# Maxima turned in one piece, phases summed with heads on partitions, the shared expert beside the logits, and another order table, in a two-layer block on one core

## Chip, core and metric

The kernel runs on one core of a Trainium2 chip. The metric is device time in microseconds (us); a median of runs is compared. Everything below in us is from the profiled execution unless it is said to be of the runs.

## What is computed

Sixteen sequences of 512 tokens with 128 features go through two layers, each an attention-like part and a mixture of experts, with a layer norm after each part. The reference, cut to what matters here:

```python
# layer 0, first part, for each of 16 heads
p1 = sum(sin(a1 * n + b1) * c, axis=-2)          # phases: 64 sines per head, 512 positions
p2 = sum(sin(a2 * n + b2) * c, axis=-2)
cross, diag, extra = exp(clip(x@k1 + p1)), exp(clip(x@k2)), exp(clip(x@k3))
num = cumsum(cross * values) * exp(p2) * extra + values * diag
den = cumsum(cross) * exp(p2) * extra + diag
x = layernorm(x + einsum(num / den, output_weight))
# layer 0, second part: the best of 8 experts per token, relu; layernorm
# layer 1, first part: 16 heads of 8 features
logits = q @ k.T * scale + pos_bias               # softmax, values, output; layernorm
# layer 1, second part
shared_out = swiglu(x, shared_gate, shared_up, shared_down)
top_id, score = argmax(x @ gate_w.T), sigmoid(max(x @ gate_w.T))
routed_out = swiglu of expert top_id on x * score
x = layernorm(x + shared_out + routed_out)
```

## The kernel before

**A list of operations and an order table.** The kernel first lists some 6,200 operations (`op(engine, cost, emit, reads, writes, delay)`), each for one engine, with the buffers that it reads and writes. `Plan.order` (L243) then runs them on a clock of its own: each engine starts the ready operation with the smallest key whose buffers are free. The key is read from `ORDER`, a string with two characters for each operation; `cost` and `delay` say how long an operation holds its engine and how long its readers wait after it. The result is the order in which instructions are emitted, engine by engine, and every engine's queue keeps that order. The costs have no other effect on the chip.

**Buffers.** Each kind of buffer has a fixed count (L331 to L365): three "pair" buffers of two PSUM banks, two "one" buffers of one bank, and in SBUF six "w2", five "p", three "mid" and eight "x", among others.

**Stages.** Sequences are taken in chunks of 2, 3, 4, 4, 2 and 1 (`CHUNKS`). For a chunk, layer 0 runs per sequence (`attention0`, with one `tile0` for each 128 tokens), then `mixture0` (logits, `route` on VectorE, a scatter of tokens into a list in DRAM, slots of 128 tokens with the weights of their expert fetched by GpSimd, a gather). Layer 1 of a chunk (`attention1`, `mixture1`) runs while layer 0 of the next chunk fills the gaps.

**Phases** (`phases`, L471). For p1 and for p2, 1024 angles (8 times 128, on partitions) times 512 positions are made in four quarters. For a quarter, ScalarE and VectorE make the angle (L484, L478), ScalarE rounds the number of turns (L491, L494), VectorE takes the turns off and clips (L499, L502), ScalarE takes the sine (L511). After all four quarters, TensorE sums: 4 blocks of positions times 8 angle blocks, with the sines as the weights and 16 columns of coefficients moving (L520), so that positions end up on partitions.

**Bias** (`slide`, L568). From a distance table a line of 1024 biases per head is made (L582 to L610), written to DRAM, and read back with every partition shifted by one (the "slid" rows, L627, 448 KB for each of 16 heads); a product turns each around (L636).

**Attention of layer 1** (`attention1`). A sequence has four groups of four heads. `spread` (L1265) sends queries and keys of a group into padded tiles: four transfers of bf16 rows and four of f32 rows. `maxima` makes rounded scores (L1286 adds the bias, L1293 the products) and takes their row maxima (ScalarE copies at L1308, VectorE halves and reduces at L1316 and L1317) into `tops[g % 2]`, of 128 queries times 4 blocks times 4 heads. `shifted` sends the negated maxima into one row of the padded queries, so that the exact scores come out shifted. `weighted` makes the exact scores (L1359), adds the bias (VectorE, L1374), takes the exponential (ScalarE, L1380), and multiplies with the values (L1389). `shifted` reads:

```python
def turn():
    for it in range(NT):
        nc.tensor.transpose(pm()[:NG, col(it)], tops[g % 2][:, it, :], ident)
# PE turn; ACT copies pm[:4, :512] to mx; then one transfer on SP:
nc.sync.dma_start(qk_pad[g % 2][D1 :: 32, 0, :], mx()[:NG])
```

**Second mixture** (`mixture1`, L1483). After `route`, GpSimd scales the tokens and scatters them; then, for each sequence of the chunk, the tokens are turned again (`transposed`, L687 and L690), go through the shared expert (L1519, `swiglu` at L1466 to L1478, L1528), are added to x (L1536) and are stored to the output (L1543). The routed experts follow in `slots` (L1554, L962, L1566), and the gathered result is added to what is read back from the output (L1578, L1583).

**Queues.** SP issues all plain transfers in order; GpSimd issues the scatters, the gathers and the fetches of weights, in order with its own arithmetic. A transfer that waits holds up all that stands behind it on its queue.

Of the kernel before, what the change touches and what calls it, by code (L numbers as in the profile page):

```python
# [18 lines left out]
P = 128  # L19
# [33 lines left out]
    "###$#P#8#N#R#H#1#6#<#B#Q#.#0#4#>#L#?#3#A#J#W#@#/#F#U#[#_#i#O#9#T#]#a#Y#Z#^#b#c#d#e#h#q#v#g#k#o#u"  # L53
    "#|$$$*$,#)#&#*#l#~$##z#y#n#}#p#I#V#`#G#E#%#,#-#S#(#M#D#X#m#s$/$2$5#w$&$;$+$1$8$@$D$G$I$K#t$-$A$F"
    "$J$N$O$P$X$]$b$e$H$T$Y$^$f$j$k$o$v$z%3%7$_$d$g$m${$~%#%&%*%-%2%8%>%@%E%I%L%O#r#K#'$i$n$p$t$y$|$}"
    "%%%(%)%.%/%0%6%:%<%A%1%4%5%;%B%F%G%J%N%P%R%V%?%C%D%K%U%X%Y%]%`%b%h%k%Q%S%T%Z%c%f%g%j%n%t%z%|&%&)"
    "&,&-&.&0&1&2&8&=&D&U&3&6&;&a&:&l&p&t&y'#')',&b'-&|'$'@'C'F'J'L&r'M'O'T'`'f'j'n'o'''p'q'u(&(+(2(5"
    "(7(=(N(Q(Z(^(O(_(e(l(t#:#2#5#7#;#C#f#j$r%$%'$E$U$Z#{$%$.$)$:$>$B$M$R$L$[$`$a$l$s$3$=$C$S$q$w$'$6"
    "$9$($7$<#x$0$4$?$Q$V$x%H%M$u%9%=$W$c$h&$%v%y#=(a(c(m(y(f(r(u(k(p(x)#(s(w)$).({):)l)o)b)k){)])a)-"
    ")3)m)5);)9)?)I)@)C)0)7)O*)*/*1)+)6)')2)%)8)/)4*J*M*R*Q*U*Y)B)F)D)J)T*o*t*x*s*u*z)H)M)K)P)Z*y*|*~"  # L60
    "*}+$+,)W)^)Q)V)d+#+*+/+&+++2)_)g)U)Y)w)}*#*'+5+9+@)p)q)i)j+'+-+)+(*T*[*_*W*Z*h*L*P*:*A*S*f*i*l*j"
    "*q*v*8*<*4*9*C+0+3+8+6+:+D*+*0)~***6+7+B+H+;+A+L*>*D*%*-*G*`*d+4+Q+V+Z)e)c)X)[+C+>+?+<+G+N+T+S+X"
    "+b)z*&*2*5*;+Y+_+a+`+d+h)u)y)r)v*(+e+k+p+g+m+{*B*F*]*a*e+x+|,$+~,',+)x)|)n)t*,+J+M+O,/,4,7+n+r+v"
    "+q+s,@,(,,,1,0,3,J,5,:,>,F,M,`,E,L,S,R,W,c,f,{-#-7-C-I-R-U-Y-g-j-n.,.4+},%-]-d,.,<,6,;,8,V,T,=,D"
    ",A,C,Q,K,r,w,x,~-(-+-0,a,d-9,p,s,X,_,y,k,o-3-<-D-T-^-a,H,I,?,Y,[,O,N,U-l-p-t-s-w-},v,z,|-'-1-x.#"
    ".+.&.-.0,],b,g,j,m.*.1.6...2.;-$-,---5-?.7.<.C.B.F.R,i,l,n,q,u-G-N-P.W.^.b-2-/-8-;.:.@.?.=.D.H.L"
    ".K.S.c-E-J-~.%.).T.[.a.Y.].h-@-F-X-`-i._.i.m.f.j.y-V-Z-M-S-b.k.s.x.o.t/(-c-h-_-f-m.9.>.J/+/2/8-)"
    "-*-6-4.u.p.q.r.v.z.}.|/$/*-:->-B-H-L/%/)/-/,///5-=-A-Q-W-[/7/;/>/</@/D.'./-u-|.5/A/E/I/H/L/R-o-r"
    "-K-O-y.P.V.~/V/`/c/./1/6/4/9/G/J/N/Q/P/T/[/U/X/Z/Y/b/h/a/g/j/i/m/q/v/x/|00070C0T0`0f0k0v0x0~1&%+"
    "%,%W%[%^%_%a%d%e%i%l%m%q%r%s%x%~&&&+%p%u%{&(&/&4&5&9&>&A&G&L&#&'&*&7&<&?&@&C&J&N&S&W&B&F&O&R&X&["  # L70
    "&^&`&c&i&m&o&s&v'('+'.'1%o%w%}&E&H&I&K&M&Q&P&T&]&V&Y&Z&_&g&j&x&{&d&h&k&q&z&}&~'&'*'/'8'>&n&u&w'%"
    "'4':';'?'B'E'['a'0'3'6'='D'G'H'K'P'W']'b'e'h'w'z'|(#&e&f'2'5'7'9'<'A'I'N'X'U'Y'Z'_'d'i't'x'R'V'^"
    "'c'm'r's'v'y'}(-(3'g'k'l'{(*(.(/(1(6(:(;(@'~(%(((0(9(<(>(A(C(J(U(V(](d(j(o(q(z(})()1)A)L)f*$)&))"
    ")G*=)=*H*K*b*g+R+W+[*?+]+f+i+t+y,9,B,^*N,G,t,}-e-k-q-v-z+l-{.$.(.G.N.X.`.d-%.e.g.l.{/&/:/?/B/O/l"
    "/p/t/z/f0%0*010@/y090G0O0Y151<1A1O1=1@1F1[1C1q1W1_1x2)1{2'20282;2>1H1P2,2:21272@2r2w2x2*1K22252Q"
    "2]2V2Z2a3,33362&323T3V3f4%3k3n404L4P4S264Q5$5(5w695}6&6@787=7B3Y:j6b6i;#;&;';);+;/;3;5;A;`;h;i;m"
    ";s;x;S;j;w;|;~<)<,#+/~0$050=0&0-020.0/06080A030D0Q0J0:0M0V0X0^0d0o0u0w1#1(0_0h0S0Z0s0I0P0[0a0n12"
    "171:0>0U0R0N0H0?0B0K1u1w1z1y2#2%0y1'0q0z1,1}2+2.2$2(2/0c0m0l0p0{24292<2=2A2K1+111)1-1;2B2D2I2H2P"
    "2U0g0j1.191J1S1X1]2Y2c2f0t0r0}0|2F2G2E2J2O2T2^2W2[2p1G1M1D1I1U2e2j2o2i2k2y181>1N1Y1g2l2s2u2q2t3)"
    "141B1?1E1^2v2z3$3#3&311$1*1L1R1b1o1t2S35393?101/16132{2|3%2~3'3*3.3-303O1V1e1`1c1j343;3A383=3U1Q"  # L80
    "1T1l1p1|3H3K3L3R3X3d1d1h1f1k1s3Q3[3_3W3]3j1r1v1Z1a2-2?2b3+3m4#4)3a3g3i3h3p443r3w3}3|4(494/474=45"
    "484A5?5C5I5G5L5T5Y5d5i5l5o5r5y5~6%64676;6?6C3^3e3l3q3o3s3t3y3v4-4*4.3~433z3x3{4O4T4>4E4W4J4M4F4I"
    "4N4m4q4R4V4x4i4n4U4Z4s5,51534$4,4&415F5H5B5D5J5N5P5O5U5p4v4|4_4c5&5V5]5_5^5b6'4D4G4b4g4l5j5u5{5s"
    "5v60464:4<4?4C6#6*6/6.62654H4K4]4`4d595>5Q686A6D4r4p4Y4[6(6,6-6)63666<6:6>6H4}5%4o4u5/6E6I6L6K6O"
    "6Z5'5*4t4w556S6W6]6a6f6j50565-525<6g6v6{6r6x7+575:5m5q5z6U6Y6[70717>4{4z4f4h6o6k6p6m757:7A797;7F"
    "6J6N6_6c6h7<7C7J7@7D7M6|7#6q6u7-7I7K7P7O7T7W6P6T6X6`6e7U7Y7^7]7c7y7/736d6l7H7L7N7Q8#8+827e7k7r7p"
    "7w7}7s8$8*7z8&8-8'8,808.838881858>8;8@8C8G8K8N8O8W8`8h8m8r8y9+9/929F7X7[7_7f7a7l7n7j7g7m7o7~7q8%"
    "7u7x7t8R8e8A8D8i8=8J8M8T8^8V8Z8?8B8d8E8P848:8U8n8s8w7{7|8)8(8789868<9-969A91989E90938p8v9:9C9G9L"
    "9J9P9V8H8L8c8g8q9K9O9R9Q9U9_8j8z8[8a9#9S9]9d9b9f9j9&9*8l8o9.9H9I9M9p9t9v8Y8]8S8Q9Y9[9a9W9e9h9m9k"
    "9y9~8}9'9)9,9>9z9}:&:#:-:9979;999=9B:0:8:=:5:;:@9<9@9g9i9n:>:G:J:B:H:V9l9q9o9s9x9|:%:':[:`:e9594"  # L90
    "8x8u:C:F:D:A:X:_:f:Z:b:r:$:)9r9w:,:g:l:n:m:q:w:(:+:.:1:<:o:u:z:s:v;,:6:?:I:M:Q:y:|:~:};%;8:O:S:L"
    ":P:U:Y:^:a;=;L;O;2;:;?;7;<;N;>;C;E;D;H;P;F;K;R;Q;U;X;V;Z;_;];c;e;g;k;n;p;r;u;}<%<*<-</<0<1<2'S'Q"
    "($('()(,(4(8(?(B(G(H(L(M(P(R(S(W([(D(I(K(Y(b(g(h(n(v(~)N)S(T(X(`(i(|),)*)<*E*I*O*X*.*3*7*@*V*^*c"
    "*k*m+o+u+w+z,&,e,h-&-.(F(E)>)E)R)`)h)s*r*w*{+=+E+F+K+P+U,P,Z+%+.+1+I,#,*,),2.3.8.n.w+^+c+j,-.M.Z"
    ".Q.U/0/3/e/o/=/C/F/K/k/s/w0#0'0;0E0L0W0]0b0e0i1%*p*n.A.E.I.O/#/'/M/S/]/W/^/_/d/n/r/{0)0,040<0F1i"
    "1m1n232X2_2h2n/u/}0+1~2C2M2N2R373:3B3I2`2d2g2m2}3(3/3>3F3u4'4+424;4@4B4e4k0(2L3<3@3E3G3M3P3J3N3S"
    "3Z3b3`3c5)5.5A5K4X4^4a4j4y4~5#5+5;5@5[5c54585=5E5`5e5f5n5t5x5|6$5M5S5X5h6+616=6B6F6M6Q6R6V6^6n6s"
    "6t6y6z6~7'72777R7h8/7%7(7d8F7E8X8_8f8k8t8|9$8I9%8{8~9?9D9N9T9^8b9X9Z9`9u9{:*:/:29(:3:4:7:R:W:c:h"
    ":k9c;4:t:x;J;M;T;W;Y::;a;[;b;q;v;{<#<&<.<B<E<I<P<?<R<V<c<n<X<r<z=g=n='=H>(>->2<3<4<8<=<5<6<9<O<<"
    "<j<7=L<><A<C<G<H<J<N<a<k<o<K<M<Q<S<U<Z<]<i<x<~<:<;<@<L<D<F<T<Y<_<`=j=<=w=}>/>=>6>9>B>F>J>N=i>K>I"  # L100
    ">M>y?6?#?.?;?R?Y?Z>$?X?L?OB#C$B)B/C+C4C;C=>QC:CGCQC}DlD'D*DtESEYE]?SI2F.F9IJIMIOIQIRITI[I_IgJ4J;"
    "JCJKJPJTJ>NwO%O-O7OCOML&O)O?ONOQOlOp<W<[<q<w<^<g<e<b<d<l<y<f<h=0=/=2<m=B=F=8=A=K=1=7<v<}=?=-=4=$"
    "=+=9=U=X<|=&=u>'>.>1=#=*<u<s<{=%=,<t>V>[>_>^>b>e=E=I=J=O=[>`>d>g>f>j>o=G=M=6=:=R>t>z>}>w>{?-=W=_"
    "=N=T=d>~?%?+?*?/?3=]=b=@=C=k=q=x={?7?:?>=Z=Y=>==?'?&?,?)?0?5?9?8?<?A=m=p=z>#>,???B?G?E?I?N=t=y>+"
    ">0>5?H?M?T?Q?V?`>:>>=|>&>E?W?c?g?]?f?k>L>R>A>D>U>Y>]?4?n?}@(=c=a=S=Q?^?_?d?b?h?l?p?o?r?y=o=s=e=l"
    "=~?s?w?{?v?x@$>)>3>4>8><?|@%@)@#@'@->h>l=`=f>q@*@.@1@7@:@?>%>*>C>G>O?C?F?j@E@^@r@9@A@H@=@B@V@C@I"
    "@N@G@J@`@P@b@i@Z@c@q@e@m@s@x@~A%A(A+A.AHAOARAXA[AbAnAsAwB=BF@2@8@<@@@F@X@U@L@M@a@g@d@T@j@f@]@_A?"
    "AEAFAIASA<A@A3A6AMA8A:A#A*A>@zA$A)A/A2AdAfAh@Y@O@R@W@l@o@p@nB(B+B-B,B0B9AeAjAPATArB5B?BDB<BABGA'"
    "A,A0A4A7BIBLBPBOBSBVAVAYAWA^AcBaBgBlBdBiBsA9A=@}A&ACB1B6B:B}C-C2ABADALAJBcBeBfBhBQBUBZB[B_C1AZAa"
    "AmAtAzC*C6C8C.C3C<A~B&B;B>BBC9C>CAC@CDCJAuA{AgAqB'CLCTCYCOCUC_BnBrApAyBxB~C&C)CeClCqAlAkA_A]CPCS"  # L110
    "CRCVCBCFCKCICMCtBqBwC0C5C7CpCzC|CuC{D,BuBzCgCkCoD&D-D0D)D+D6CZCbCaCfCiD.D5D;D2D9DBBYB^BKBNB`CsCv"
    "CxDJD[D`D8D=DAD<D>DUDMDSD]DYDcDsD_DfDjDeDgDxDhDpDuDwD|E$E)EKEcEgEjEnErE|F)F/F;F>FBFPD3D7E*E-D?DG"
    "DDDHDEDbDOD^DRDKDaDIDLE&E+D{D~E.E/E2E,E0E9E<E@E6E:EME3E7EPEWEZEeEsEwDXDTDVDPDnDrDoDmF5F@FFF=FAFK"
    "DvDyD}E%E(FEFMFQFLFNFSE8E=ECEJEUFOFTFWFRFUF]EEELEIEREfFVFZFaF`FeFlE[EaE?EDEkF'F6F:FtFzF~EAEBETEV"
    "F^F_FcF[FbFgFvFkFqG#ElEoEuEzF#FpFwG&FuFxG*F8F<EqExFDF}G'G/G%G)G6EXE^EyE}F*G(G+FYG1G3G@E_EhEiEmEv"
    "FIFJFmGDGHGLE`EdEQENG2G$G,G.G4G8G<G;GdGFF?FCF0F4FHG=GCGGGAG>GMF,F2F(F-F7GEF{GJGIGNGWE{F$FfFjFoGK"
    "GOGRGQGTG]E~F&F%F+F3FyG-G9GSGoH:GUGXG_G[GbG|GfGaGgGeGuH/GjGrGxH$H+H9H6H*H3H5H;GzHDHIHKHZHcHgHmHx"
# [88 lines left out]
class Plan:  # L206
# [8 lines left out]
    def op(self, engine, cost, emit, reads=(), writes=(), delay=None):  # L215
        if delay is None:
            delay = (0.25, 0.12, 0.15, 0.15, 3.4)[engine]
# [104 lines left out]
def block_kernel(ctx: ExitStack, tc: tile.TileContext, d, out: bass.AP):  # L322
# [148 lines left out]
    def phases(lin):  # L471
        for which in range(2):
            sines = []
            for quarter in range(4):
# [21 lines left out]
                def reduced(arg=arg, turns=turns):  # L496
# [15 lines left out]
                    writes=[arg],  # L512
                )
                sines.append(arg)
            acc = buf("one", f"phase{which}")

            def sums(acc=acc, sines=sines):
                for t in range(NT):
# [1340 lines left out]
```

## Time and profile before

| | |
|---|---|
| median of 3 runs | 2387.21 us (2380.75 to 2396.14) |
| the profiled execution, its own time | 2306.71 us |
| its span, first to last instruction | 2305.0 us |
| mean granted TensorE clock | 0.966 |
| busy: PE, PEld | 2123.2 us (92%), 1086.2 us (47%) |
| busy: DVE, ACT, POOL | 1805.3 us (78%), 1468.9 us (64%), 759.6 us (33%) |
| moved by DMA | 180.03 MB, 78 GB/s on average |

PE is TensorE, PEld its loading of weights, DVE VectorE, ACT ScalarE, POOL GpSimd, SP the engine that only issues transfers. A group's line gives its line in the kernel, engine, operation, output and inputs with their shapes, and how many; then its busy time, the mean of one in ns, and the idle time of the engine in front of it with what ended it. An f32 product shows as two records. The busy time of TensorE counts overlapping instructions once.

### The profile page before, as it was taken

The page shows a single profiled execution, that of the slowest core. Times are in us where ns is not written, and L with a number is a line of the kernel's source. Part 1 is how long each engine was busy: PE and PEld are TensorE (multiplying, and loading weights), DVE is VectorE, ACT ScalarE, POOL GpSimd, SP SyncE. Part 2 cuts the span into 40 slices and gives each one's busy share as a digit, 9 for nine tenths or more (in the row PEclk, how much of TensorE's full clock was granted, in tenths as well). Part 3 has the DMA queues.
Part 4 walks back from the last instruction along what each step waited for, and adds up shares of the span by engine and source line. Part 5 has one row for each costly group of instructions (what it writes and reads, how often), then busy time and mean ns, then how long its engine had stood idle before and what let it go on. Part 6 is the DMA issues. An engine that isn't in the chain of part 4 may idle for free. (4 is left out here: it accounts for less than half of the span.)

```text
span 2305.0 us, 34824 instructions
## 1 busy us (share of the span) xinstructions
PE 2123.2 (92%) x12723; PEld 1086.2 (47%) x12820; DVE 1805.3 (78%) x3286; ACT 1468.9 (64%) x1848; POOL 759.6 (33%) x763
## 2 busy tenths in 40 slices
PE   5898989999999998999999998999999999998994
PEld 4465744444545445454443443455534334544353
DVE  6355698788879787888878687988887999687973
ACT  6322367866576784667567876557687876676651
POOL 1134552134121425621214234422231424223524
PEclk9898999999999998999999998999999999999997
DMA  6522321211210333320102331212232211432334
GB/s 178 158 91 71 92 70 42 69 45 49 77 45 11 85 111 93 97 87 10 41 14 67 105 105 28 74 52 79 73 86 71 68 38 56 135 116 74 111 106 145
DMA packets 152446, 180.03 MB, mean 78 GB/s; under 512 B 19332, under 2 KB 125444, under 8 KB 152276
## 3 DMA queue, kind: packets, MB, share of 16 engines
q1 hardware_dynamic: 125588, 84.27, 13.7%
q0 software_dynamic: 26688, 93.53, 13.7%
q8 instruction: 101, 1.65, 0.3%
q14 instruction: 69, 0.57, 0.1%
HBM read 127.67 MB, written 42.93 MB: 74 GB/s over the span
## 5 line engine op out<-in xcount | busy, mean ns | idle before, releaser
L1380 ACT ACTIVATE p<-p 128x1024 f32<-128x1024 f32 x512 | 537.4, 1058 | 237.1 <-DVE p L1374 222.3
L1374 DVE TENSOR_TENSOR p<-st,bias 128x1024 f32<-128x1024 f32 x512 | 604.3, 1217 | 90.4 <-PE st L1359 80.3
L1308 ACT CAST low<-s 128x1024 bf16<-128x1024 f32 x512 | 495.0, 1020 | 113.6 <-PE s L1293 91.1
L823 POOL DMA_INDIRECT ws<-tab,rows x212 | 215.7, 1017 | 460.4 <-PE py L962 168.0
L1316 DVE TENSOR_TENSOR low<-low 128x1024 bf16<-128x1024 bf16 (+1 forms) x512 | 299.5, 585 | 78.7 <-ACT low L1308 69.8
L1359 PE MATMUL st<-qk_pad 32*128 32x512 f32 x2048 | 319.5, 646 | 3.9 <-DVE p L1374 3.6
L1286 PE MATMUL s<-bias,ident 128*128 128x512 bf16 x927 | 301.6, 398 | 10.3 <-ACT low L1308 3.2
L1389 PE MATMUL av<-p,vaug 128*32 128x512 f32 x2048 | 282.3, 609 | 7.6 <-ACT p L1380 6.2
L1067 POOL TENSOR_TENSOR self<-ev,own 128x1024 f32<-128x1024 f32 x64 | 125.3, 1957 | 429.1 <-DVE ev L1061 309.6
L1293 PE MATMUL s<-qk_pad 32*128 32x512 bf16 x1024 | 204.2, 391 | 24.0 <-issue 14.7
L1317 DVE TENSOR_REDUCE tops<-low 128x4 f32<-128x512 bf16 x256 | 175.5, 686 | 10.4
L1293 PEld LDWEIGHTS <-qk_pad 32*128 32x128 bf16 x1024 | 48.9, 91 | 244.0 <-issue 227.5
L823 POOL DMA_INDIRECT yg<-results,place x128 | 128.3, 1002 | 95.3 <-issue 38.3
L1359 PEld LDWEIGHTS st<-qk_pad 32*128 32x128 f32 x2048 | 93.6, 184 | 128.6 <-DVE p L1374 44.8
L1286 PEld LDWEIGHTS <-ident 128*128 128x128 bf16 x1024 | 75.1, 100 | 145.8 <-issue 142.7
L1083 PE MATMUL cum<-ev,tri 128*128 128x512 f32 x256 | 132.0, 640 | 10.5 <-DMA ev<-carry 8.6
L1114 PEld LDWEIGHTS y<-ow,ot 128*128 128x128 f32 x1024 | 122.7, 194 | 32.1 <-issue 19.2
L1114 PE MATMUL y<-ow,ot 128*128 128x128 f32 x1024 | 130.0, 281 | 2.1 <-DVE cnt L808 1.3
L1048 PE MATMUL pv<-vw,xt 128*128 128x512 f32 x256 | 128.1, 625 | 0.0
L962 PE MATMUL py<-ws,h 128*128 128x128 f32 x848 | 111.2, 285 | 9.3 <-DVE h L1478 5.2
L1061 DVE TENSOR_TENSOR ev<-pv,ex 128x1024 f32<-128x1024 f32 x64 | 78.0, 1219 | 52.8 <-PE pv L1048 25.9
L962 PEld LDWEIGHTS py<-ws,h 128*128 128x128 f32 x848 | 102.1, 196 | 36.7 <-issue 14.5
(191 smaller groups left out, 2903.4 us busy)
## 6 DMA issues: line engine op xcount, KB each, us to landing
xq<-tokens SPq DMA_DIRECT2D x44, 256.0 KB
results<-yq SPq DMA_DIRECT2D x44, 256.0 KB
qk_pad<-qk SPq DMA_DIRECT2D x256, 32.0 KB
slid<-line SPq DMA_DIRECT2D x16, 448.0 KB
tokens<-zero SPq DMA_DIRECT2D x4, 1472.0 KB
x<-in_x SPq DMA_DIRECT2D x16, 256.0 KB
xt<-in_xt SPq DMA_DIRECT2D x16, 256.0 KB
qk_pad<-qk SPq DMA_DIRECT2D x256, 16.0 KB
```

The source lines that it names most:

```text
L823: nc.gpsimd.indirect_dma_start(out, bass.IndirectOffsetOnAxis(to, 0) if to is not None else None, in_, bass.IndirectOffsetOnAxis(of, 0) if ...
L962: nc.tensor.matmul(py()[:, col(s)], h()[:, c, col(s)], ws[s]()[:, off + c * W : off + (c + 1) * W], start=(c == 0), stop=(c == 1),)
L1114: nc.tensor.matmul(y()[:, :P], ot()[:, hf, col(c)], ow[:, 4 * hf + c, :], start=(hf == 0 and c == 0), stop=(hf == 1 and c == 3),)
L1286: nc.tensor.matmul(s()[:, i, :], ident16, bias16[:, 4 * g + 2 * jp + i, 2 * u + 1 : 2 * (u + N) : 2], start=True, stop=False,)
L1293: nc.tensor.matmul(s()[:, i, :], pad[r, 0, col(it)], pad[r, 1, :], start=False, stop=True,)
L1308: lambda s=s, jp=jp, part=part: nc.scalar.copy(part(0, N)[:, 2 * jp : 2 * jp + 2, :], s()),
L1316: nc.vector.tensor_tensor(part(0, n), part(0, n), part(n, 2 * n), ALU.max)
L1317: nc.vector.tensor_reduce(tops[g % 2][:, it, :], part(0, N // 4), AX.X, ALU.max, negate=True)
L1359: nc.tensor.matmul(s[jp]()[:, i, :], pad[r, 1, col(jt)], pad[r, 0, :], start=True, stop=True,)
L1374: lambda jp=jp, h=h, pj=pj: nc.vector.tensor_tensor(pj(), s[jp](), bias[:, h : h + 2, u : u + N], ALU.add),
L1380: ACT, 1.0, lambda pj=pj: nc.scalar.activation(pj(), pj(), AF.Exp),
L1389: nc.tensor.matmul(acc()[32 * j : 32 * j + 32, :], va[:, jt, h * VW : h * VW + 32], p[j // 2]()[:, j % 2, :], start=(jt == 0), stop=(jt == ...
```

## The change

Four edits and a new table.

1. *Maxima.* One transpose for all 16 columns of `tops` (4 blocks times 4 heads), a copy of 16 partitions by 128 columns, and four transfers on SP, one for each block.
2. *Phases.* The coefficients are the weights and 512 positions move, so that the 16 heads are on partitions; each quarter is added as soon as its sines are there. ScalarE copies the sum and four small transposes bring positions back to partitions. For the odd quarters GpSimd rounds the turns, in two instructions, in ScalarE's place.
3. *Shared expert.* It stands in `shared`, which is called with the turned tokens of `logits`, for each sequence right after its logits. Its sum goes to a "mid" buffer, which is stored; x itself stays as it was until GpSimd scales it.
4. *Order.* `ORDER` is new for all operations, and several costs and delays are changed, which act through the order alone. `mx` is two smaller buffers.

```diff
-            delay = (0.25, 0.12, 0.15, 0.15, 3.4)[engine]
+            delay = (0.13, 0.11, 0.12, 0.1, 3.4)[engine]
...
-        "mx": (wp, [P, N], F32, 1),
+        "mx": (wp, [P, P], F32, 2),
...
+                def whole_too(arg=arg, turns=turns):
+                    nc.gpsimd.tensor_scalar(turns(), arg(), INV2PI, ROUND, ALU.mult, ALU.add)
+                    nc.gpsimd.tensor_scalar(turns(), turns(), ROUND, None, ALU.subtract)
+                if quarter % 2:
+                    op(POOL, 4.0, whole_too, reads=[(arg, 0), (arg, 1)], writes=[turns])
+                else:
+                    op(ACT, 2.3, whole, reads=[(arg, 0), (arg, 1)], writes=[turns])
...
-                for t in range(NT):
-                    for j in range(8):
-                        nc.tensor.matmul(
-                            acc()[:, t * H0 : (t + 1) * H0],
-                            sines[j // 2]()[:, j % 2, t * P : (t + 1) * P],
-                            cblk[:, j, :],
-                            start=(j == 0), stop=(j == 7),
-                        )
-            op(PE, 8.0, sums, reads=[*sines, "cblk"], writes=[acc])
+            for quarter, sines_of in enumerate(sines):
+                def add(acc=acc, arg=sines_of, quarter=quarter):
+                    for j in (2 * quarter, 2 * quarter + 1):
+                        nc.tensor.matmul(
+                            acc()[:H0], cblk[:, j, :], arg()[:, j % 2, :], start=(j == 0),
+                            stop=(j == 7),
+                        )
+                op(PE, 3.0, add, reads=[sines_of, "cblk"], writes=[acc])
...
+                    nc.tensor.transpose(
+                        acc()[:, t * H0 : (t + 1) * H0], sums()[:H0, col(t)], ident[:H0, :H0]
+                    )
...
-                for it in range(NT):
-                    nc.tensor.transpose(pm()[:NG, col(it)], tops[g % 2][:, it, :], ident)
+                nc.tensor.transpose(
+                    pm()[:rows, :P], tops[g % 2].rearrange("p i j -> p (i j)"), ident
+                )
...
-                lambda: nc.sync.dma_start(qk_pad[g % 2][D1 :: 32, 0, :], mx()[:NG]),
-                writes=[("shift", g % 2)], delay=2.4,
+            for it in range(NT):
+                    lambda it=it: nc.sync.dma_start(
+                        qk_pad[g % 2][D1 :: 32, 0, col(it)],
+                        mx()[NG * it : NG * it + NG, :P],
+                    ),
+                    writes=[("shift", g % 2, it)], delay=2.4,
...
+    def shared(b, x, xt):
+        pg, pu = buf("pair", f"pg_s{b}"), buf("pair", f"pu_s{b}")
...
+        h = swiglu(pg, pu, NT, f"s{b}")
+        py, kept = buf("one", f"py_s{b}"), buf("mid", f"kept_{b}")
...
+                kept(), py(), 0.5, x(), ALU.mult, ALU.add
...
+            SP, 0.45, lambda: nc.sync.dma_start(xout[b], tok(kept())), reads=[kept],
...
-            xt = transposed(x, f"{n}_{i}", [("scaled", c, i)])
-            pg, pu = buf("pair", f"pg_{n}_{i}"), buf("pair", f"pu_{n}_{i}")
...
-            logits(x, gw, "gw", lg, i, f"l1_{b0 + i}")
+            shared(b0 + i, x, logits(x, gw, "gw", lg, i, f"l1_{b0 + i}"))
```

## Prediction

> **What bounds the kernel now.** I read the page's header first, then the busy time of each engine cut into stretches at the events that separate the work (first transfer of slid rows landed, first rounded score, last attention product, end), then TensorE's waits inside the long stretch, then the groups that the diff touches, and the timeline of the start and of the end. The stretches (window, its length, busy time and instructions of PE, PEld, DVE, ACT, POOL; then granted clock, DMA share, GB/s):
>
> ```profile
> 0.00:67.00 67.00, 37.58 (x153) 30.85 (x154) 36.87 (x44) 39.85 (x41) 7.79 (x39) 0.88 0.73 188
> 67.00:306.00 239.00, 210.18 (x1050) 143.69 (x1051) 139.09 (x287) 70.73 (x105) 103.06 (x85) 0.93 0.30 91
> 306.00:2224.00 1918.00, 1830.49 (x11233) 871.91 (x11328) 1598.39 (x2864) 1345.22 (x1682) 613.66 (x600) 0.98 0.25 71
> 2224.00:2305.00 81.00, 44.99 (x292) 39.72 (x290) 30.93 (x92) 13.16 (x20) 35.12 (x39) 0.80 0.42 128
> ```
>
> TensorE stands idle for 29 us in the first 67, for 29 in the next 239, for 88 in the 1918 of the middle (busy 95%), and for 36 in the last 81: 182 in all. The next engine in the middle, VectorE, is busy 83%. So the middle is TensorE's, the start and the end are chains of waits. TensorE's waits in the middle (engine, line, releaser, us in total, times, longest):
>
> ```profile
> PE s L1293 <- issue: 14.7, 90, 0.4
> PE s L1293 <- DMA qk_pad<-qk: 9.3, 12, 2.3
> PE av L1389 <- ACT p L1380: 6.2, 8, 1.7
> PE st L1359 <- DVE p L1374: 3.6, 3, 2.1
> ```
>
> No single wait is worth over 15 us, so only less work on TensorE, or a better order all along, can shorten the middle. The groups that the change touches (busy, mean ns | idle before):
>
> ```profile
> L1331 PE MATMUL pm<-ident,tops 128*4 128x128 f32 x256 | 40.0, 277 | 4.9 <-DVE tops L1317 2.6 <-DVE cnt L808 1.7 <-ACT xqt L943 0.4
> L687 PE MATMUL pt_m<-ident,x 128*128 128x128 f32 x64 | 12.0, 319 | 1.0 <-ACT xt_m L690 1.0
> L520 PE MATMUL phase<-cblk,arg 128*128 128x16 f32 x128 | 26.3, 360 | 3.1 <-ACT arg L511 3.1
> ```
>
> **The change part by part**, in us of the profiled execution (2306.71, span 2305.0).
>
> *Maxima.* In each of 64 groups four transposes become one: 192 of 256 go. By busy time that is 192 x 40.0/256 = 30. [...]
>
> ```profile
> 1453.07 0.60 PE L1331 MATMUL pm<-ident,tops 128*4 128x128 f32 x4
> 1453.51 1.02 PE L1519 MATMUL pg_m<-xt_m,wgs 128*128 128x512 f32 x2
> ```
>
> The four show as 0.60 busy, but the next product starts 0.44 after them, 0.11 each. So I take 64 x 3 x 0.11 = 21 and keep 30 as the far end. ScalarE's copy of maxima (570 ns for 512 columns, 569 mean) shrinks to 128 columns; the nearest row of that width, the 128x128 activation of L1176, has 382 ns, small 32-column ones 0.19. I take 0.3: 17 off ScalarE, hidden (70% busy in the middle).
>
> *Four transfers for one.* SP's issue of this transfer takes 510 to 558 ns, so the last of four leaves 3 x 0.53 = 1.6 later; less 0.3 from the copy and 0.3 from the transposes, +1.0 on the chain from maxima to scores. The chain is 0.28 (transpose) + 0.2 + 0.3 + 2.1 (issues) + landing. The landing is not shown for it; the neighbour transfer into the same pad takes 2.0, 2.3, 3.5 and 5.1 where the chain of waits names it. At 2.3, the nearest in the middle of these, the chain needs 5.2; at 5.1, 8.0. Its cover: in the order of the built program I summed the TensorE work, each product at its group's busy time over its count, between the turn and the first score that needs it. Before: shortest 5.2, median 20.5. After: 6.5, 6.9, 7.2, 7.4, 7.6 are the shortest, median 22.8. So mostly nothing is paid, and a handful of 64 groups pays up to 1: +3 (0 to +12). Behind the four on SP's queue wait the spreads of the next group, stores of results and fetches of slots; SP already stands 194.9 at this line waiting for the copy, and 192 more issues are 102 of its 2305. That the spreads come 1.6 later is inside the same covers.
>
> *Shared expert.* It moves from the start of each mixture to behind the logits and uses their transposed rows: 64 transposes and 16 copies (9.5 on ScalarE) go. By start-to-start time 64 x 0.11 = 7, by busy time 12; I take 8. Its products, VectorE's 3 instructions per image, and its store (one SP issue, 0.38) are as many as before. Input rows are freed sooner; a "mid" buffer of three is held for a product, an add and a store.
>
> *Phases.* 64 products with 128-column weights become 16 of 512 columns and 8 small transposes. Per 512-column product the row of L1519 gives 33.1/32 = 1.03, so 16.5 + 8 x 0.15 = 18 for 26: -8. More matters how they lie: before, each set of 32 stands whole on TensorE's queue and holds back until its last sine (27.1 to 40.9, 46.0 to 61.6), and only behind it come the slid rows, which landed at 66.8 behind 3.5 MB of tables and zeros. After, each quarter is added when ready, the line of biases is made from a product in the middle of the phases, and four slid transfers go straight behind it, ahead of the tables. Worked out: VectorE starts its reductions at about 11 and has 8 x (2 x 1.22 + 0.69) + 3 = 28 to do, to 39; a sine, two products, a copy, the turn and the clip end the phases at 44 at best. The distance table is behind 6 MB; at the 211 GB/s of the first 20 us it lands at 28, dist and its copy at 31.5, the line at 35, slid rows at 40. Half of the rounding goes to GpSimd, eight instructions between 0.94 (its memset of that size) and 1.96 (its two-input row, L1067). [...] while GpSimd wrote its constants,
>
> ```profile
> 4.17 5.46 DVE L478 TENSOR_SCALAR arg<-lin,ab 128x512 f32<-128x512 f32 x3 [2.37 <-DMA ab<-in_ab]
> 9.68 0.98 DVE L478 TENSOR_SCALAR arg<-lin,ab 128x512 f32<-128x512 f32 x2
> ```
>
> three cost 5.46, later two cost 0.98. [...] if all of 8 x 0.94 to 8 x 1.96 is added, at 52 to 60. I take 48: much of it lies in VectorE's gaps. At 66.8 before had done 7.3 of the later work (5.4 pv, 1.9 scores); the same state then comes at 55: -12 (-18 to 0). By the order, 5 more of other work stands ahead of the first rounded score: the front gives -7, the middle loses 5.
>
> *End.* After the last attention product stands 35 of TensorE work, not 43 (row prices): one slot group's pg, pu and py (6) now precede it. Then the scatter: before, four weight fetches at 1.25 held it from 2244.2 to 2248.3; after, only a fetch of results that can start at about 2240 does, so it starts near 2245.3. The weights then come later, so 3 of it remains at most at the last slots: -3 (-6 to +4).
>
> *Order table.* Middle: -21 - 8 + 6 - 5 = -28 of work, at 95% busy -29. The new table is made with costs and delays nearer the rows (prefixes 1.80, slots 2.75). From a score product to the value product that needs it the order leaves, by the same sums, 3.7 at the 2nd percentile for 3.2, and the bunches of four shared experts are spread out. A tenth of the middle's 88 idle: -8 (-40 to +40; no row prices an order).
>
> Sum: -7 - 29 + 3 - 8 - 3 = -44: 2306.7 to 2262.7. The median of the runs shown is 2387.21, 1.035 times the profiled one, and nothing here says why; I scale: 2341.
>
> **The rivals.**
> 1. *The order packs tighter.* Idle in the middle falls by 45 and busy time is the right price (-13 more): 2306.7 - 44 - 37 - 13 = 2212.7, scaled 2290. For: 88 idle in many small waits. Against: VectorE at 83% would come to 86%.
> 2. *Slots stay empty.* TensorE's saved time becomes waits for VectorE and ScalarE (80.3 and 69.8 are VectorE's own waits, in lockstep): a third of 29 remains: -7 - 10 - 3 = -20: scaled 2366.
> 3. *It does not do what it says.* GpSimd's contention takes the start's gain, tables behind the slid rows delay the first slots, and the removed transposes were under others: 0 to -10: 2377 to 2387.
> 4. *Slower: the four transfers come late.* Place: first scores of each group. If the cover by rows is an overestimate and each group waits the 1.6 of the three added issues, 64 x 1.6 - 47 = +55: scaled 2444. It decides from (47 + 23)/64 = 1.1 per group on. Against: covers of 6.5 and more.
>
> **How the numbers follow.** Forecast 0.53 (own range 2322 to 2358), tighter 0.17, empty slots 0.17, nothing 0.07, late transfers 0.06. About 1% is what a measurement of this kernel can tell from no change. Under 2363.3: 0.53 + 0.17 + 0.08 = 0.78; over 2411: 0.06; between: 0.16. The range 2288 to 2374 leaves out the late transfers, half of the nothing and the far end of the tight order.
>
> **What would show it.** In the profile after: TensorE's busy time down by 40 to 50 from 2123.2; the turn at 64 instead of 256 instructions, about 10 busy; the first rounded score near 300 instead of 308; p2e near 50 instead of 61.6; no wait of st for the maxima's transfers beyond 5; idle in the middle 70 to 95. Wrong if st waits on those transfers in the tens of us, if VectorE's reductions at the start take twice 2.48, or if the idle of the middle moves by over 30 either way.

## The result, and the profile after

The changed kernel takes 2373.19 us in the median of 20 runs (2362.43 to 2383.14), the kernel before 2386.24 on the same chip (20 runs, 2366.96 to 2399.67): ratio 0.9948, 95% interval 0.9927 to 0.9969. That is 13 us where 46 were forecast. Which chip it was turned out to matter, so the chips have letters here:

| chip | before | changed kernel | ratio (95%) |
|---|---|---|---|
| A, first comparison | 2386.24 | 2373.19 | 0.9948 (0.9927 to 0.9969) |
| B | 2304.88 | not run | |
| C | 2388.32 (2403.51 at another time) | 2376.44 | 0.9952 (0.9935 to 0.9969) |
| D | 2387.62 | 2373.63 | 0.9916 (0.9885 to 0.9947) |
| E | 2302.59 | 2302.04 | 0.9995 (0.9980 to 1.0009) |

Which chip A was is not on record; it can be C or D. The profile that the prediction read (2306.71) is like those of B and E, the runs beside it like those of A, C and D. On E, where the kernel before is as fast as it was in that profile, the change is worth nothing. How far to trust such ratios: the kernel before against itself gave 1.0018 (0.9998 to 1.0038) on B and 0.9955 (0.9928 to 0.9982) on D, so half a per cent can come from nothing.

In the profiled execution of the changed kernel on A (2366.07, span 2364.4) the header has

```profile
PE 2130.7 (90%) x12476; PEld 1055.1 (45%) x12476; DVE 1807.8 (76%) x3286; ACT 1425.7 (60%) x1824; POOL 786.2 (33%) x771
```

which cannot be set against 2123.2 of before, since the clocks differ (0.953 and 0.966). The groups that the change touches are as the diff has them (busy, mean ns | idle before):

```profile
L1526 PE MATMUL py_s<-wds,h_s 128*128 128x128 f32 x256 | 36.1, 299 | 11.1 <-DVE h_s L1504 10.5 <-DVE o L1437 0.4 <-DVE cnt L828 0.3
...
L530 PE MATMUL phase<-arg,cblk 128*16 128x512 f32 x32 | 18.4, 706 | 25.3 <-ACT arg L521 25.3
L1352 PE MATMUL pm<-ident,tops 128*16 128x128 f32 x64 | 17.3, 276 | 0.8 <-DVE tops L1337 0.6
L543 PE MATMUL phase<-ident,sums 16*128 16x16 f32 x8 | 1.0, 241 | 0.0
```

Turns of maxima: 64 for 256. The phases cost 18.4 + 1.0 for 26.3, as forecast. New is the 10.5 that the shared expert's last products wait for VectorE. On the timeline a lone turn stands 0.11 ahead of the next product, the start-to-start price of the prediction:

```profile
1519.58 0.27 PE L1352 MATMUL pm<-ident,tops 128*16 128x128 f32 x1
1519.69 0.61 PE L1306 MATMUL s<-bias,ident 128*128 128x512 bf16 x2
```

**Like with like.** The stretches of before on B and of the changed kernel on E, cut at the same events as in the prediction, the middle from first rounded score to last attention product (columns as there: window, length, busy time of PE, PEld, DVE, ACT, POOL, granted clock, DMA share, GB/s). Before:

```profile
0.00:67.00 67.00, 39.34 (x153) 32.00 (x154) 36.58 (x44) 39.85 (x41) 7.78 (x39) 0.87 0.69 186
67.00:307.40 240.40, 210.82 (x1059) 144.04 (x1059) 141.33 (x295) 72.02 (x107) 103.44 (x85) 0.94 0.30 91
307.40:2221.00 1913.60, 1845.97 (x11343) 875.07 (x11343) 1596.89 (x2856) 1344.40 (x1682) 612.42 (x600) 0.98 0.25 71
2221.00:2300.50 79.50, 42.62 (x270) 37.69 (x269) 30.85 (x92) 12.05 (x19) 35.10 (x39) 0.76 0.42 130
```

After:

```profile
0.00:67.00 67.00, 35.01 (x82) 10.71 (x83) 43.01 (x47) 33.08 (x37) 25.30 (x47) 0.95 0.78 206
67.00:298.70 231.70, 211.22 (x1070) 144.37 (x1069) 140.95 (x309) 69.05 (x104) 105.07 (x87) 0.93 0.31 90
298.70:2221.20 1922.50, 1830.62 (x11096) 858.80 (x11095) 1591.06 (x2841) 1312.44 (x1668) 619.48 (x602) 0.97 0.25 71
2221.20:2299.60 78.40, 35.80 (x231) 31.20 (x231) 28.47 (x90) 9.84 (x15) 32.42 (x36) 0.77 0.38 120
```

The front is 8.7 shorter (307.4 to 298.7), the end 1.1 (79.5 to 78.4), and the middle 8.9 longer, where 34 less was forecast. In the middle TensorE's busy time falls by 15.4 (1845.97 to 1830.62), but its idle time rises by 24.3 (67.6 to 91.9) and its clock falls from 0.98 to 0.97. These are two single executions on two chips. Two variants of the changed kernel on E (one transfer, three aside, below) have nearly the idle time of this one over their whole spans, 187 and 189 for 187; before on B has 162.

### The profile page after: what moved, and what is told of

Its sections match the earlier page's. It is cut to its first block, busy times and chain, and to the rows that moved or that the text cites. A ratio compares the mean times of both kernels' runs of the same rounds, so it can differ in the third digit from the quotient of the medians.

```text
span 2364.4 us, 34535 instructions
## 1 busy us (share of the span) xinstructions
PE 2130.7 (90%) x12476; PEld 1055.1 (45%) x12476; DVE 1807.8 (76%) x3286; ACT 1425.7 (60%) x1824; POOL 786.2 (33%) x771
## 3 DMA queue, kind: packets, MB, share of 16 engines
q1 hardware_dynamic: 127124, 84.28, 13.6%
## 4 chain that ended last, share of the span: by engine, by line
PE 47%; DVE 19%; issue 5%; ACT 4%; DMA 2%; POOL 2%; SPq 1%; another core or an unknown queue 1%; DVEq 0%; POOLq 0%; ACTq 0%
PE st L1385 8%; PE av L1415 7%; PE s L1306 6%; DVE p L1400 5%; PE s L1313 4%; DVE low L1336 3%; PE py L982 3%; DVE tops L1337 2%; PE y L1134 2%; PE cum L1103 1%; PE pv L1068 1%; PE ph L1186 1%; PE pg L1579 1%; ACT p L1406 1%; ACT low L1328 1%
## 5 line engine op out<-in xcount | busy, mean ns | idle before, releaser
L1306 PE MATMUL s<-bias,ident 128*128 128x512 bf16 x1024 | 326.1, 400 | 30.3 <-ACT low L1328 15.6
L1336 DVE TENSOR_TENSOR low<-low 128x1024 bf16<-128x1024 bf16 (+1 forms) x512 | 294.7, 576 | 76.4 <-ACT low L1328 62.2
L1415 PE MATMUL av<-p,vaug 128*32 128x512 f32 x2048 | 281.4, 612 | 21.0 <-ACT p L1406 15.4
L685 POOL TENSOR_SCALAR rs<-mv 128x4 f32<-128x4 f32 x64 | 23.0, 359 | 414.3 <-DVE mv L680 408.2
L1115 DVE TENSOR_TENSOR o<-cum,gg 128x1024 f32<-128x1024 f32 x64 | 78.1, 1221 | 64.1 <-PE cum L1103 41.0
```

The costliest lines, as they stand in the source:

```text
L1306: nc.tensor.matmul(s()[:, i, :], ident16, bias16[:, 4 * g + 2 * jp + i, 2 * u + 1 : 2 * (u + N) : 2], start=True, stop=False,)
L1336: nc.vector.tensor_tensor(part(0, n), part(0, n), part(n, 2 * n), ALU.max)
L1415: nc.tensor.matmul(acc()[32 * j : 32 * j + 32, :], va[:, jt, h * VW : h * VW + 32], p[j // 2]()[:, j % 2, :], start=(jt == 0), stop=(jt == ...
```

## Experiments

Each is told with the ratio to before on its own chip. A new order table can't be put on other operations as it is. So in the runs of single parts, operations that are in both kernels keep the place of the table that is named, and new ones are put behind their neighbours; where only the body of an operation changes, every other instruction stands where it stood.

### Was the profile of before a typical one? (B, D)

> The kernel before, unchanged. Theory A (the profiled execution from which the sum was made, 2306.71 at a granted clock of 0.966 with 927 records of the bias products instead of 1024, was not a typical one): a new profiled execution takes 2370 to 2400 at a clock of 0.944 to 0.957, the 80 us more lie in the long middle stretch, and TensorE's busy time comes out above 2140 instead of 2123. Rival (profiled executions of this kernel are simply like that): again 2300 to 2315 at 0.966. The ratio to the kernel before is 1.000 in either case and shows what a measurement can tell.

Measured: 2307.56 (22 runs), profiled 2302.17 at 0.963, with all 1024 bias products recorded. Theory A falls: on B such an execution is typical. That the profile and the runs beside it came from different chips is the plain reading; its chip is not on record.

> A profile of the kernel before on the chip of this call. If before takes about 2388 there: the 80 more than in the profile that the prediction read lie in standstills of ScalarE, VectorE and SP in which the trace names no releaser (60 or more of TensorE's idle time in gaps above 1.7, against 37), in the second half of GpSimd's runs of indirect transfers, and not in longer instructions. If about 2305: as the first repetition, 2290 to 2320.

Measured on D: 2379.56 (10 runs); the profiled execution (2394.70, span 2393.0) was the slowest of them. VectorE's and SP's waits there, with releaser, total, times, longest:

```profile
DVE ex L985 <- remote: 19.0, 1, 19.0
```

```profile
SPq L1265 <- remote: 26.5, 3, 11.7
```

and ScalarE's:

```profile
ACT low L1308 <- remote: 15.8, 6, 3.8
ACT xt_m L690 <- remote: 8.1, 1, 8.1
```

"remote" is a wait in which the trace names no releaser on this core. The trace of before on B has none at all. All twelve traces of A, C and D have such waits, all eight of the fast chips (the prediction's profile among them) have none. Busy times of ScalarE and VectorE agree within 0.2% (1470.4 and 1468.3, 1807.5 and 1805.7). From 2198 on, ScalarE and VectorE stand still together for 8.1 while GpSimd issues its indirect transfers without a pause. TensorE's gaps above 1.7 us after the first 70 sum to 91 on D and 37 on B. The execution profiled on D is 92 longer than the one on B. TensorE stands idle for 58 of that (219.8 for 161.7) and is busy for the other 34 (2173.1 for 2138.7), with 258 us at half rate for 169. So standstills, some of them in GpSimd's long runs of indirect transfers, are the larger part, and a lower clock of TensorE the rest. What makes the standstills is not known.

### The maxima alone, in the order of before (B, C, D)

```diff
-                for it in range(NT):
-                    nc.tensor.transpose(pm()[:NG, col(it)], tops[g % 2][:, it, :], ident)
+                nc.tensor.transpose(pm()[:rows, :P], tops[g % 2].rearrange("p i j -> p (i j)"), ident)
...
-                lambda: nc.sync.dma_start(qk_pad[g % 2][D1 :: 32, 0, :], mx()[:NG]),
+                lambda it=it: nc.sync.dma_start(qk_pad[g % 2][D1 :: 32, 0, col(it)], mx()[NG * it : NG * it + NG, :P]),
```

> The kernel before with the maxima edit alone (one transpose, a small copy, four transfers on SP in the place of one), every other instruction in the same place on every queue. The prediction's price (192 transposes at 0.11 less, 3 for late transfers): -18, ratio 0.992. If the slots stay empty (TensorE then waits for VectorE and ScalarE instead): -6 to 0, ratio 0.997 to 1.000, and TensorE's idle time of the middle up by about as much as its busy time falls. If the four transfers come late in an order that was not made for them: above 1.005, with waits of st for qk_pad in the tens of us.

Measured: 2312.70, ratio 1.0023 (1.0000 to 1.0047), at a mean clock of 0.9594 against 0.9639 of before. The turn's group shrank as planned. Waits for the spread transfers rose from 6.0 to 11.6, in a profiled execution (2326.51) that was the second slowest of 22:

```profile
PE s L1255 <- DMA qk_pad<-qk: 11.6, 10, 1.9
...
PE st L1327 <- DMA qk_pad<-mx: 1.2, 1, 1.2
```

The edit, with the order in place, gains nothing. The rows of maxima themselves are hardly waited for (1.2).

```diff
-                for it in range(NT):
-                    nc.tensor.transpose(...)
+                for again in range(4):
+                    for it in range(NT):
+                        nc.tensor.transpose(...)
```

> The kernel before with each group's four transposes of maxima done four times over (768 transposes more, same result, one transfer, same order). It asks what such a transpose is worth on TensorE. At the start-to-start price of 0.11: +84, ratio 1.035. At the busy price of 40.0/256: +120, ratio 1.050. If TensorE's time is not what sets the middle (the work falls into its waits): under +40, ratio below 1.017.

Measured: 2358.36, ratio 1.0224 (1.0191 to 1.0258): +53, 0.07 for each of 768, at a clock that rose to 0.9688. So added work costs two thirds of the start-to-start price of 0.11, and the edit that removed work did not pay. The sum used one price for both directions.

The next two keep three idle transposes beside the one (four transfers), and take one transfer instead of four (with the columns of `tops` laid out by head, then block).

> The kernel before with the maxima edit alone, but three idle transposes kept beside the one (so TensorE's work is as before; ScalarE's small copy and the four transfers are in). With the maxima edit alone, 2313 at a clock of 0.959 against 2305 at 0.964 was measured. If the loss there came from late transfers: 2318 to 2330 at an unchanged number of half-rate stretches. If it came from the clock (theory B): back at the time of before within 6, at 0.962 to 0.966.

Measured on C: 2409.93, ratio 1.0085 (1.0057 to 1.0113), clock 0.9424 against 0.9455. It is not within 6 of before, as the clock theory had it. It is 0.0062 above the ratio of the edit without these transposes, some 15 us for 192 of them, though on another chip. So 1.0023 may be a saving of some 15 and a cost as large of the rest of the edit (the small copy, the four transfers) in this order; no run on one chip separates the two.

> The kernel before with one transpose, the small copy and one transfer, in the order of before (SP's queue as before, 192 transposes and 17 of ScalarE less). By the transposes' price from the fourfold run (0.07 each) and theory C: -10 to -16, ratio 0.993 to 0.996. If saved TensorE work does not count because its waits or its clock eat it: ratio 0.998 to 1.003, with the clock down by 0.003 or more as it was with four transfers (0.959 for 0.964).

Measured on D: 2385.30, ratio 0.9992 (0.9970 to 1.0014). With four transfers or one, the maxima alone gain nothing. Beside the profile of before on D, TensorE's idle time is the same (219.2 for 219.8), and so is its busy time (2171.8 for 2173.1), with 192 transposes fewer: 299 us at half rate for 258.

### The shared expert alone (B)

`mixture1` loses its loop over the sequences, `shared` is called behind `logits`, as in the change; the table of before.

> The kernel before with the shared expert beside the logits alone; its 128 operations are put in the order table behind the neighbours that they have in the changed kernel's table, all else keeps its relative order. The prediction's price (64 transposes and 16 copies less): -8, ratio 0.997. If the place matters more than the transposes (products bunched where scores were smooth, a pair of PSUM banks taken from the scores): up to +15, ratio 1.000 to 1.006, with more waits of s and st.

Measured: 2495.47, ratio 1.0821 (1.0783 to 1.0859), clock 0.938. Both expectations were far off. Its waits grew everywhere (av for ScalarE's p 27.1 for 6.2, rows fetched for the experts 20.8 for 8.0). A place that was not worked out together with the rest costs 190; the price of 64 transposes can't be seen beside it.

### The changed kernel again, and with its work put back (C, D)

> The changed kernel, unchanged, beside the kernel before on one chip. Theory B (the clock): the traces so far show that TensorE runs at half rate for one or more stretches of 3.41 us[...]; the kernel before has 49 such stretches (167 us, 0.963), and taking work out of TensorE's queue without closing its waits makes more of them. Then the mean clock of the changed kernel is 0.004 to 0.012 below that of the kernel before on the same chip, it has 58 to 70 half-rate stretches, and the ratio is 0.990 to 0.998. Rival (the first comparison was peculiar to its chip, the sum was right): ratio 0.978 to 0.984 at an equal clock.

Measured: 2376.44, 0.9952 (0.9935 to 0.9969). The clock is 0.9484 against 0.9455: on this chip it rose, against theory B, though the ratio is in the range that theory B gave.

```diff
+                for it in range(1, NT):
+                    nc.tensor.transpose(pm()[:NG, col(it)], tops[g % 2][:, it, :], ident)
...
+                if w is wg:
+                    for j in range(NT):
+                        nc.tensor.transpose(ph()[:, 0, col(j)], xt()[:, col(j)], ident)
```

> The changed kernel with 256 transposes on TensorE put back as idle work: 3 more in each group of maxima, 4 in front of each shared expert's first product, results unused, all else as it is. At the 0.07 each that the fourfold transposes showed, or 0.11 as the prediction has it: 18 to 28 slower than the changed kernel. If the saved transposes had been filler that kept the clock up (theory B): within 8 of the changed kernel, at a clock that is 0.003 to 0.006 higher.

Measured: 2388.46, ratio 1.0008 (0.9986 to 1.0030): +12 to the changed kernel, 0.05 for each of 256, at 0.9494. Read the other way, in the new order taking these 256 out is worth 12 on C, and with them back in nothing is left of the change's gain there.

> The changed kernel again, as the neighbour of the two above and of a profile of before on the same chip. On a chip on which before takes about 2388: ratio 0.9948 to 0.9955 as twice before. On one where before takes about 2305 (no waits without a releaser in its trace): 0.980 to 0.985 if the gain is the sum of the prediction and the slow chips hide it; 0.995 to 1.003 if part of the gain on the slow chips comes from meeting fewer of these waits.

Measured on D: 2373.63, 0.9916 (0.9885 to 0.9947), a little lower than the 0.9948 to 0.9955 expected.

### Four transfers, one, or three aside (C, D, E)

```diff
-                    lambda it=it: nc.sync.dma_start(qk_pad[g % 2][D1 :: 32, 0, col(it)], ...),
+                    lambda it=it: it == 0 and nc.sync.dma_start(
+                        qk_pad[g % 2][D1 :: 32, 0, :].rearrange("h (i n) -> h i n", i=NT), mx()[:rows, :P]),
```

> The changed kernel with the columns of the maxima laid out by head and then by block, so that the same one transpose and one small copy can be sent by one transfer instead of four; SP issues 192 fewer, all else in place. Theory C (the four transfers cost about 20 in the order of before, where keeping the three idle transposes left +20 and taking them away +7; the score products wait for spreads that stand behind them on SP): 5 to 20 below the changed kernel, ratio to before 0.986 to 0.994. Rival (the new table was made for four transfers and waits only 1 for them): within 4 of the changed kernel.

Measured on D: 2349.99 (5 runs), 0.9834 (0.9801 to 0.9866), 24 below the changed kernel there. It looked like the missing part. For the three aside, `it > 0` sends `mx` to a DRAM tile `aside[b, g, it]`:

> The changed kernel in which one transfer brings all maxima to the scores and the three others carry the same bytes to a place in DRAM that nothing reads; SP issues as many as in the changed kernel. If the cost of the four is SP's queue (what stands behind them comes later): as the changed kernel, ratio to before 0.991 to 0.996. If it is the landing of the last of four that the exact scores wait for: as with one transfer, 0.982 to 0.986.

Measured on C, where before now took 2403.51: 2373.83, 0.9881 (0.9850 to 0.9913). On E all three ran side by side:

> The changed kernel, as the neighbour of the next two on one chip: ratio to before 0.991 to 0.996 where before takes 2380 to 2405. On a chip where before takes about 2305: 0.980 to 0.985 by the prediction's sum, 0.995 to 1.003 if part of the gain elsewhere comes from meeting fewer standstills.

> The changed kernel with one transfer again. If the four transfers cost what the first comparison showed: 15 to 28 below its neighbour with four. If that was the spread between measurements: within 8 of it.

> One transfer for the maxima and three sent aside, again. If the landing of the last of four is the cost: within 6 of the run with one transfer. If SP's queue is: within 6 of the changed kernel. If both share it: halfway.

Measured: four 2302.04 (0.9995), one 2305.43 (1.0007, 0.9990 to 1.0023), three aside 2301.74 (0.9993, 0.9974 to 1.0012). Theory C falls: on this chip the four transfers cost nothing that can be measured. The lead of 24 on D was not tried again there; it is not explained.

### The phases (C)

> The kernel before with the edit of the phases alone (coefficients as weights, a product per quarter as its sines come, four small turns, GpSimd rounding the odd quarters); the order of all else, the slid rows too, is as before. The prediction's price: -8 of TensorE work, of which the start keeps 5, ratio 0.997 to 0.999; p2's exponentials near 50 to 55 instead of 61.6. If GpSimd and VectorE disturb each other: reductions of VectorE well above their 1.22, p2's exponentials after 60, ratio 1.000 or above. Theory B adds: the half-rate stretches from 50 to 70 (six of them in before) become one to three, up to -8.

Measured: 2387.38, 0.9983 (0.9964 to 1.0002), clock 0.9475 for 0.9455: -4 by the ratio. In the next, `if quarter % 2` is made false, so that ScalarE rounds all quarters:

> The changed kernel with one transfer for the maxima, and with ScalarE rounding all quarters of the phases as before (GpSimd none), each instruction in the place that the table gives it. The traces show the pairs of reductions at 4.02 beside GpSimd's rounding and 2.46 without, and the clip at 1.17 for 0.69. If that contention is what delays the start: no reduction above 2.6, p2's exponentials before 60 instead of 64, and 2 to 8 below the run with one transfer (ratio to before 0.980 to 0.983). If ScalarE becomes the bound of the start in turn: p2's exponentials at 62 or later and no gain.

Measured: 2373.17, 0.9878 (0.9849 to 0.9908). All pairs of reductions take 2.46 to 2.48, and still p2 is turned at 65.4, not earlier than with GpSimd (63.8 to 65.9 in four traces of C and D, 63.5 on E). The slowing beside GpSimd's rounding (4.02 a pair with it) is real and was not the limit.

> The kernel before with the maxima turned at once and sent by one transfer, and with the edit of the phases, in the old order; the shared expert where it was. If the parts add up as measured alone (-2 and -4): ratio 0.996 to 0.999, and then the shared expert's place with the new table carries 30 of the 37 that the changed kernel with one transfer gains. If the parts were masked alone: 0.985 to 0.993.

Measured: 2394.47, 0.9968 (0.9951 to 0.9985): -8, about the sum of the two. What the shared expert's place and the new table add was not separated further; on C the runs that have both lie 4 to 22 below this one by their ratios.

## Why the prediction was wrong

**The scaling.** 2341 is 2262.7 times 1.035, and "nothing here says why". The runs suggest it: profile and runs came from two kinds of chips. A sum made on the one was scaled to the other as if all its parts stretched alike. What stretches from B to D are standstills (37 to 91 us of long gaps) and time at half rate (169 to 258), not the work of ScalarE and VectorE (within 0.2%).

**The idle time that was read.** The first of the prediction's waits, 14.7 in 90 for "issue", is at the products behind the bias products, and of those only 927 of 1024 were recorded. The trace of B with all 1024 has no such wait, and 67.6 idle in the middle for 88. So the tenth for the table was taken of a number that was in part missing records. The signs did not warn either: 91.9 after lies within the 70 to 95 that they allowed, though it is 24 more than before.

**Front and end held, roughly.** Forecast -7 and -3, measured -8.7 and -1.1 in this pair. The first rounded score came at 301.3 to 308.4 in five profiles with the old front on fast chips and at 298.5 to 303.3 in three with the new one, so 8.7 is known to no better than some 5. And the front's reason was wrong at one point: p2e was to come near 50 and came at 65. The changed kernel on E:

```profile
13.19 4.02 DVE L502 SCALAR_TENSOR_TENSOR arg<-turns,arg 128x1024 f32<-128x1024 f32 x2
14.25 3.62 POOL L513 TENSOR_SCALAR turns<-turns 128x1024 f32<-128x1024 f32 x1
17.25 1.17 DVE L505 TENSOR_SCALAR arg<-arg 128x1024 f32<-128x1024 f32 x1
...
26.71 2.46 DVE L502 SCALAR_TENSOR_TENSOR arg<-turns,arg 128x1024 f32<-128x1024 f32 x2
...
52.99 0.57 ACT L537 COPY sums<-phase 16x512 f32<-16x512 f32 x1
60.27 3.33 PE L656 MATMUL turn_ps<-slid,flip 128*128 128x448 f32 x4 [6.59 <-DMA slid<-line]
63.52 0.61 PE L543 MATMUL phase<-ident,sums 16*128 16x16 f32 x4
...
64.83 0.21 DVE L465 TENSOR_SCALAR p2e<-phase 128x64 f32<-128x64 f32 x1
```

The reductions beside GpSimd's rounding take 4.02 a pair instead of 2.46, so the slowing that the prediction weighed is there; GpSimd's eight instructions take 17.5 together, for 7.5 to 15.7 allowed. But the sums of p2 are ready at 53.6, and their small turns stand on TensorE's queue behind the fourth slid turn, which waits for its rows until 60.3. The prediction asked when the sines end, and not what stands ahead of the step after them.

**The step that failed: "at 95% busy -29", and with it the tenth of the idle for the table.** On B and E, the middle by the terms of the sum (half-rate time is from the trace's record of the clock, 81.9 and 109.2 us; half of it is taken as lost, an estimate):

| | forecast | measured |
|---|---|---|
| TensorE work at full rate | -28 | -29 (busy -15.4, less 13.6 for 27.3 more at half rate) |
| the same work at half rate | 0 | +13.6 |
| idle: share of 95%, table, late transfers | -1 - 8 + 3 | +24.3 |
| sum | -34 | +8.9 |

Counting only the part of half-rate time in which TensorE is busy gives -31 and +15.5, the same picture. So the work was priced rightly. On E it did not become time: it was handed back as waits and as a slower clock, which the sum put at nothing. This is rival 2, slots that stay empty, in a stronger form: it left a third of the middle's 29, on E nothing was left. (On C, 256 of the transposes are worth 12 where their price of 0.11 makes 28, so there part of it became time.) The waits of the middle, after:

```profile
PE s L1313 <- DMA qk_pad<-qk: 10.9, 7, 2.7
PE po L1126 <- DVE o L1119: 9.7, 4, 3.4
PE av L1415 <- ACT p L1406: 9.5, 17, 1.2
PE pt_l L707 <- DVE x L693: 7.4, 3, 4.6
PE py_s L1526 <- DVE h_s L1504: 5.7, 3, 5.2
PE s L1306 <- DVE p L1400: 5.1, 5, 2.4
```

and before on B:

```profile
PE av L1389 <- ACT p L1380: 6.2, 8, 1.7
PE s L1293 <- DMA qk_pad<-qk: 6.0, 7, 1.6
PE st L1359 <- DVE p L1374: 3.6, 3, 2.1
PE pm L1331 <- DVE tops L1317: 3.4, 5, 1.3
```

No single one explains it. The plain reading is that TensorE arrives earlier at VectorE, ScalarE and the spreads, which come as late as before. The largest, po, was 0.2 in the middle and 11.8 in the front before (1.4 there now): part of the front's gain is that wait, moved. That the edit of the maxima gains nothing is shown with the order held fixed (1.0023 and 0.9992); whether its saving was handed back or paid for its own copy and transfers is not separated. For the shared expert and the table the handing back is argued from these rows: the one cost 190 in the old order, the other was not run by itself.

**The clock was missing from the sum.** By the traces TensorE's granted clock is 1.00 or 0.50, and each holds for 3.41 us or a multiple of it (3.41 to 17.07 at 0.50 on A). The changed kernel on E, at one wait of 1.18:

```profile
1465.16 0.63 PE L1306 MATMUL s<-bias,ident 128*128 128x512 bf16 x2
...
1466.04 0.62 PE L1306 MATMUL s<-bias,ident 128*128 128x512 bf16 x2
1467.84 0.41 PE L1313 MATMUL s<-qk_pad 32*128 32x512 bf16 x2 [1.18 <-DMA qk_pad<-qk]
1468.18 1.03 PE L1306 MATMUL s<-bias,ident 128*128 128x512 bf16 x2
...
1469.69 1.03 PE L1306 MATMUL s<-bias,ident 128*128 128x512 bf16 x2
...
1481.91 0.63 PE L1306 MATMUL s<-bias,ident 128*128 128x512 bf16 x2
```

```profile
1464.67:1468.08 3.41, 2.23 (x12) 0.51 (x10) 2.46 (x4) 1.93 (x2) 2.92 (x2) 1.00 0.49 132
1468.08:1471.49 3.41, 3.41 (x11) 0.59 (x10) 3.38 (x16) 2.21 (x3) 1.40 (x2) 0.50 0.30 46
...
1478.30:1481.70 3.40, 3.40 (x14) 1.96 (x12) 2.07 (x12) 2.01 (x3) 1.80 (x2) 0.50 0.20 25
1481.70:1485.10 3.40, 3.40 (x24) 2.19 (x22) 1.97 (x5) 2.03 (x3) 2.26 (x3) 0.99 0.41 120
```

Busy 2.23 of 3.41, then four stretches at 0.50, in which a pair of bias products takes 1.03 for 0.62. Counted from start to start, two pairs (bias and scores) take 1.51 for 0.88, so by estimate some 6 of these 13.65 us are lost, behind a wait of 1.18. Busy time alone does not tell when this happens: in the profiled execution of the changed kernel on A the 33 falls to half rate followed stretches busy from 0 to 76%, yet behind one of 1.58 in 3.41 (from 1970.16) the clock stayed at 1.00; and 10 half-rate stretches there that were busy throughout, like the first three of these four on E, were followed by another. Over 43 runs of before on B the time follows the mean clock with a correlation of -0.95, 19 us for each 0.01; a longer wait can lengthen a run and lower its clock at once, so this slope holds both. By it the 0.0055 between before and the changed kernel on E (0.9653, 0.9598) go with 10 us, and the 0.0045 of the maxima alone with 9. On C and D the changed kernel's clock was the higher one (0.9484 for 0.9455, 0.9487 for 0.9459), so the fall does not come with the edit on every chip.

**The other rivals.** Nothing speaks for tighter packing: idle time in the middle moved by 24 in the other direction. Late transfers: in the new order they cost no more than the priced +3, since four and one agree on E; st waits about 1 us for these rows. "It does nothing" has the right size on E, by none of the reasons given.

**What stays open.** Why the change gains 12 to 14 on A, C and D and nothing on E. The gains on A and C are no larger than what before once showed against itself (0.9955), but they came three times in the same direction. On D before has lost 83 us against B by its last rounded score; the changed kernel has lost 72 against E on D (in the slowest of its runs there), 57 on C and 50 on A. Waits without a named releaser, summed over VectorE, ScalarE and SP (some overlap), come to 70 to 109 in the five traces of slow chips with the old order and to 39 to 69 in the seven with the new one. So the changed kernel meets fewer standstills there; that this is its gain fits, but was not shown. Nor was it shown that the chip makes the difference and not the time at which it was used: before took 2388 and later 2403 on C. No version beat both kernels on every chip.

## What to carry to other kernels

Removing work from an engine that is 95% busy need not pay: here it paid between nothing (E) and 12 of a price of 28 (C). Ask whether the next instruction's inputs are ready earlier too, run the saving alone in the old order before pricing it, and don't take the price of added work (0.05 to 0.07 here) for that of removed work. Price a wait with the clock that follows it: look at the granted clock in windows behind each wait (one of 1.18 was followed by four stretches at half rate). Count an engine's records before its idle time is read. And before scaling a profile to a median, see that both are of the same chip.

## What the runs showed of the hardware

- The same program took 2303 and 2305 on two chips and 2386 to 2403 on others, with equal busy times of VectorE and ScalarE (within 0.2%), standstills without a named releaser on the slow ones (waits of 70 to 109 us in the traces with the old order), and more of TensorE's time at half rate (258 us on D, 169 on B).
- TensorE's granted clock was 1.00 or 0.50, in stretches of 3.41 us. Half rate followed stretches that were busy to 38% (1.31 of 3.42 on B) or 65% (2.23 of 3.41 on E), but not one that was busy to 46% (1.58 of 3.41 on A). On E it ended behind a full stretch (3.40 of 3.40, to 1481.70), but three full ones before that did not end it.
- GpSimd's rounding and VectorE's reductions took longer side by side: 4.02 for 2.46 a pair, the clip 1.17 for 0.69, GpSimd's second instruction 3.62 for 2.77 (A).
- One transfer took 16 partitions of 128 into 4 rows of 512 as well as four transfers did (2305.43 and 2302.04 on E).
- A transfer that waited held up SP's queue: in the profile that the prediction read, SP waited 72.2 at L904 for `tokens`, and issued nothing from 122.6 to 194.9.
